# Score units of an attention kernel that end with the diagonal, and other places for its small pieces

## The chip, the cores and the metric

The kernel runs on one core of a Trainium2 chip. The metric is the device time of one execution in microseconds. Engines go by the names of the profile: PE is TensorE's matmul, PEld its weight load, DVE VectorE, ACT ScalarE, POOL GpSimd, SP SyncE.

## The reference

Input x has 2 batches of 1024 tokens with 256 channels; all is float32. An attention layer and a feed-forward layer follow each other, each added to its input and then normalised:

```python
q = (x @ Wq)  # 16 heads of 16 channels
k, v = x @ Wk, x @ Wv  # 4 heads of 16 channels, each used by 4 query heads
att = q @ k.T / 4 + slope[head // 4] * (key_pos - query_pos)
att = softmax(where(key_pos <= query_pos, att, -inf))
x = layernorm(x + (att @ v) @ Wo)
# top-1 of 8 experts (256 -> 512 -> 256, gated by silu), plus a shared expert
x = layernorm(x + shared(x) + routed(x))
```

The change concerns the attention part alone.

## The kernel before

**Tiles.** There are 2 batches of 8 query tiles (qt 0 to 7) with 128 tokens each, and key tiles of the same size. For a query tile only the keys up to its own tile count; the tile with the same number as the query tile holds the diagonal, where a part of the keys is masked.

**Two passes over the scores.** The row maximum of the softmax is taken out before the exponential, and the kernel needs it early. So it computes the scores twice.

- *S* (start_s, line 388, and end_s, line 411): queries in the partitions, keys in the free dimension, for the maximum alone. The result is reduced along the keys on VectorE into `past` (line 417). The block on the diagonal goes through the mask first: for one half of the key/value heads VectorE takes the minimum with `causal` into `diag` (line 427), for the other half ScalarE copies the block (line 435) and POOL masks it (line 438). Some slots later VectorE reduces `diag` (line 449, 128 x 1024).
- *T* (start_t, line 480, and end_t, line 494): keys in the partitions, queries in the free dimension. ScalarE evicts it with the exponential into `pT` (line 504), or, on the diagonal, copies it to `pD` (line 507), POOL masks it (line 509), and ScalarE takes the exponential later (line 521).

Between the two, join_maxima (line 456, VectorE) brings the partial maxima of a query tile together in `mneg`, and spread_maxima (line 466) turns them with four transposes (mT, line 470) and adds them to the queries on VectorE (qS, line 474).

**Units.** The S work of a query tile is cut into units (s_units, line 376): a unit is 4 key/value heads x 512 columns, that is one block of keys for all 4 query heads of a group, or two blocks for two of them, or four blocks for one. A unit with one block takes four S matmuls of 128 columns for each key/value head, one with two blocks two of 256, one with four blocks one of 512. Before the change the diagonal block is a unit by itself, and comes first.

**Steps and bursts.** The loop at line 854 goes through 72 steps, one for each pair of a query tile and a key tile. A step has two bursts: each runs two T matmuls (512 columns) and the S matmuls of two key/value heads in four row groups of the array at once, issued in turn (run, line 744). The S unit is ten steps ahead of T (LEAD): ten units run before the loop, between the projections, and the last ten steps have no S and run the pieces of the shared expert in between. Every matmul of T and S has a PSUM bank of its own from a pool of six (`ps_st`); a burst takes four.

**Slots and gaps.** After each burst stands a gap (line 795), with a running number, the slot: even slots follow the first burst of a step, odd ones the second; slots below zero are those of the lead. A gap holds, in this order: deferred work whose slot has come (after_burst), then on TensorE a product yT with the values if one is due (line 529, four matmuls, mostly in even gaps), then the transposes of maxima if the slot fits, then small pieces. The small pieces finish a query tile (finish, line 546): yq transposes the result and VectorE normalises it to y_n, ytp transposes that, o_ps multiplies it with Wo, x1tp transposes the output of the layer norm, lg makes the router's logits. They, and mT, use one bank together (`ps_m`, one buffer). Each has a cost; a gap has room 6, a product takes 4 of it, the maxima 4, and a piece its own cost and 2.

All engines but SP run in the order of the code in this part, since the schedule is manual.

Of the kernel before, what the change touches and what calls it, by code (L numbers as in the profile page):

```python
# [12 lines left out]
ALU = mybir.AluOpType  # L13
# [3 lines left out]
P = 128  # L17
N_HEAD = 16
N_KV = 4
REP = N_HEAD // N_KV  # L20
# [24 lines left out]
def attn_moe_postln_kernel(  # L45
# [15 lines left out]
    nc = tc.nc  # L61
# [9 lines left out]
    HALF = N_KV // 2  # L71
# [89 lines left out]
    causal = acon.tile([P, P], F32, tag="causal", name="causal")  # L161
# [101 lines left out]
    with (  # L263
# [111 lines left out]

        def s_units(b, qt):

            units = [(0, REP, qt, 1)]
            done = 0
            while done < qt:  # L380
                n = 4 if qt - done >= 4 else 2 if qt - done >= 2 else 1
                units += [(r, 4 // n, done, n) for r in range(0, REP, 4 // n)]
                done += n
            return [(b, qt, *u) for u in units]

        rowmax, parts = {}, {}

        def start_s(unit, h, j):
            b, qt, r0, nr, key, n = unit
            if (b, qt) not in rowmax:  # L390
                rowmax[b, qt] = (
                    mp.tile([P, N_KV, REP, P], F32, tag="diag", name="diag"),
                    mp.tile([P, N_KV, REP, 4], F32, tag="past", name="past", bufs=6),
                )
                parts[b, qt] = {qt: 0}
            parts[b, qt].setdefault(key, len(parts[b, qt]))
            g = h * HALF + j
            rows = slice(g * PAD, (g + 1) * PAD)
            sp = bank("s_ps")
            return sp, [  # L400
                lambda r=r: nc.tensor.matmul(  # L401
                    sp[:, r * n * P : (r + 1) * n * P],
                    lhsT=qT[b][rows, r0 + r, ts(qt, P)],
                    rhs=kT[b][rows, key * P : (key + n) * P],
                    start=True,
                    stop=True,
                )
                for r in range(nr)
            ]

        def end_s(unit, h, sp, last):
            b, qt, r0, nr, key, n = unit
            diag, past = rowmax[b, qt]
            gs = slice(h * HALF, (h + 1) * HALF)
            if key != qt:
                for j in range(HALF):
                    nc.vector.tensor_reduce(  # L417
                        past[:, h * HALF + j, r0 : r0 + nr, parts[b, qt][key]],
                        sp[j].rearrange("p (r k) -> p r k", r=nr),
                        AX.X,  # L420
                        ALU.max,
                        negate=True,
                    )
                return
            if not last:
                for j in range(HALF):
                    nc.vector.tensor_tensor(  # L427
                        diag[:, h * HALF + j],
                        sp[j].rearrange("p (r k) -> p r k", r=REP),
                        causal.unsqueeze(1).broadcast_to([P, REP, P]),  # L430
                        ALU.min,
                    )
            else:
                for j in range(HALF):
                    nc.scalar.copy(  # L435
                        diag[:, h * HALF + j].rearrange("p r k -> p (r k)"), sp[j]
                    )
                nc.gpsimd.affine_select(  # L438
                    out=diag[:, gs],
                    in_=diag[:, gs],  # L440
                    pattern=[[0, REP * HALF], [-1, P]],
                    compare_op=ALU.is_ge,
                    fill=MASKED,
                    base=0,
                    channel_multiplier=1,
                )
            at(
                slot + (1 + last if slot < 0 else 2 + 2 * last),
                lambda: nc.vector.tensor_reduce(  # L449
                    past[:, gs, :, 0], diag[:, gs], AX.X, ALU.max, negate=True  # L450
                ),
            )
# [3 lines left out]
        def join_maxima(b, qt):  # L456

            past = rowmax.pop((b, qt))[1]
            nc.vector.tensor_reduce(
                mnegs[qt % 2][:, :, :, ROW_MAX].rearrange("p r g -> p g r"),  # L460
                past[:, :, :, : len(parts[b, qt])],
                AX.X,
                ALU.min,
            )
# [264 lines left out]
        steps, first = [], {}  # L729
# [4 lines left out]
        slot = 0  # L734
        deferred, posts, products = [], [], []
# [4 lines left out]
        def at(when, what):  # L740

            deferred.append((when, what))
# [10 lines left out]
        def after_burst():  # L753
            for d in [d for d in deferred if d[0] <= slot]:
                deferred.remove(d)
                d[1]()
# [8 lines left out]
        def pieces(room, gap_cost=2):  # L765

            while room > 0:
                for p in posts:
                    if p[0] <= slot and p[2][0] <= room:
                        room -= p[2][0] + gap_cost if p[2][0] else 0  # L770
                        advance(p)
                        break
                else:
                    return

        def maxima():
            n = 0
            for k in order:
                if slot == 2 * first[k] - 3:
                    join_maxima(*k)  # L780
                if slot == 2 * first[k] - 2:
                    spread_maxima(*k)
                    n += 1
            return n
# [10 lines left out]
        def gap(room):  # L795
            nonlocal slot
            after_burst()
            start_route(True)
            if products and products[0][0] <= slot:
                product(*products.pop(0)[1])  # L800
                room -= 4
            room -= 4 * maxima()
            pieces(room)
            slot += 1

        def wide_gap():

            nonlocal slot
            after_burst()
            start_route(False)  # L810
            if products and products[0][0] <= slot + 1:
                product(*products.pop(0)[1])
            if not maxima():
                pieces(4, 4)
            slot += 1
            if tail:
                tail.pop(0)()
            after_burst()
            if not maxima():
                pieces(4, 4)  # L820
            slot += 1
# [21 lines left out]
        slot = -LEAD  # L843
# [10 lines left out]
        for n, (b, qt, kt) in enumerate(steps):  # L854
            last = n + 1 == len(steps) or steps[n + 1][:2] != (b, qt)
# [6 lines left out]
            if s_queue:  # L862
                unit = s_queue.pop(0)
                for h in range(2):

                    t, s = [], []
# [9 lines left out]
            else:  # L876

                t = [[start_t(b, qt, kt, h, j) for j in range(HALF)] for h in range(2)]
# [18 lines left out]
    with (  # L897
# [291 lines left out]
        h = shared(2)  # L1189
# [6 lines left out]
        for e in range(E):  # L1196
# [3 lines left out]
            else:  # L1200
                j = e + 2 - E
                rows[E + j] = fetch(E * OWN + j, 1)
            n = OWN if e + 1 < E else 1
# [8 lines left out]
            k = 4 if e == 0 else 3 if e < 3 else 2  # L1212
# [33 lines left out]
        with tc.If(n > SOON):  # L1246
            for j in range(SOON, NO):
# [3 lines left out]
                k = E + j  # L1251
# [45 lines left out]
```

## Time and profile before

| | |
|---|---|
| median of 3 runs | 600.9 us (600.33 to 602.37) |
| the profiled execution | 602.41 us, span 600.7 us |
| PE busy | 572.7 us, 95% of the span, 3708 instructions |
| DVE busy | 344.4 us, 57%, 734 instructions |
| ACT busy | 267.0 us, 44%, 484 instructions |
| POOL busy | 155.4 us, 26%, 189 instructions |
| mean granted clock of TensorE | 0.988 |
| lead (S and projections) | up to about 65 us |
| steps with S and T | about 65 to 348 us |
| steps with T alone, shared expert, router | about 348 to 450 us |
| experts | from about 450 us |

A float32 matmul appears as two instructions, one for each pass. In the chain and the timeline a line gives the start and the length in us, the engine, the tile that is written and the line of the kernel; a window's line gives its bounds, its length, then the busy time of PE, PEld, DVE, ACT and POOL with the number of instructions, TensorE's clock, the DMA share and GB/s. A group's line gives the busy time and the mean of one in ns, then the idle time before it with what ended that.

### The profile page before, as it was taken

What the parts mean: (1) busy time and instruction counts of PE and PEld (TensorE: products, weight loads), DVE (VectorE), ACT (ScalarE), POOL (GpSimd) and SP (SyncE); (2) the same over time, 40 slices, a digit from 0 to 9 for tenths busy, and PEclk for the clock granted to TensorE, in tenths of its full rate; (3) what the DMA queues carried; (4) which work ended last, traced back from release to release, by engine and by line L of the source; (5) the groups of instructions that cost most, each with busy time, mean ns of one, the idle gap of its engine ahead of it and who ended that gap; (6) DMA issues with size and microseconds to landing.
All of it is one profiled execution on the core that took longest, in us unless ns stands there. A gap on an engine that the chain in (4) does not pass through costs nothing.

```text
span 600.7 us, 9431 instructions
## 1 busy us (share of the span) xinstructions
PE 572.7 (95%) x3708; PEld 327.8 (55%) x3708; DVE 344.4 (57%) x734; ACT 267.0 (44%) x484; POOL 155.4 (26%) x189
## 2 busy tenths in 40 slices
PE   7999999999999999999999999999999999999990
PEld 4555534444445353435356644645664788888650
DVE  3186767867776767777766845342541264444541
ACT  1433476676665656655575754554112111111120
POOL 4010222111111102013321120232111237766541
PEclk9999989999999999999999999999999999999996
DMA  9700000000000000000100000100163545752100
GB/s 311 245 1 2 2 0 2 1 1 1 2 2 1 1 1 0 3 0 28 45 1 1 3 0 1 39 33 1 35 215 98 181 160 187 242 180 79 48 19 4
DMA packets 23104, 32.66 MB, mean 54 GB/s; under 512 B 3294, under 2 KB 18948, under 8 KB 23056
## 3 DMA queue, kind: packets, MB, share of 16 engines
q1 hardware_dynamic: 18784, 25.28, 12.7%
q0 software_dynamic: 3456, 6.34, 3.0%
q8 instruction: 31, 0.51, 0.4%
q10 hardware_dynamic: 816, 0.39, 0.2%
q14 instruction: 17, 0.14, 0.1%
HBM read 22.20 MB, written 12.97 MB: 59 GB/s over the span
## 4 chain that ended last, share of the span: by engine, by line
PE 87%; DVE 7%; ACT 1%; DMA 1%; issue 1%; POOL 0%; POOLq 0%; ACTq 0%
PE t_ps L485 18%; PE yT L529 11%; PE s_ps L401 11%; PE gu_sh L688 6%; PE qpj L294 5%; PE gp L1108 5%; PE dp L1124 5%; PE up L1108 5%; PE dp_sh L708 4%; DVE past L417 3%; PE o_ps L574 2%; PE mT L470 2%; DVE past L449 1%; PE lg L599 1%; PE dp L1166 1%; PE gp L1016 1%
## 5 line engine op out<-in xcount | busy, mean ns | idle before, releaser
L401 PE MATMUL s_ps<-kT,qT 32*128 32x128 f32 (+2 forms) x1280 | 184.0, 378 | 1.2 <-DVE past L417 0.7
L417 DVE TENSOR_REDUCE past<-s_ps 128x1 f32<-128x512 f32 (+2 forms) x224 | 144.6, 686 | 61.6 <-PE s_ps L401 44.9
L485 PE MATMUL t_ps<-qS,kT 32*128 32x512 f32 x576 | 173.7, 637 | 0.6 <-ACT pD L507 0.6
L504 ACT ACTIVATE pT<-t_ps 128x512 f32<-128x512 f32 x224 | 121.6, 600 | 93.2 <-PE s_ps L401 65.0
L401 PEld LDWEIGHTS s_ps<-kT,qT 32*128 32x128 f32 x1280 | 96.2, 185 | 14.4 <-ACT pT L504 4.5
L485 PEld LDWEIGHTS t_ps<-qS,kT 32*128 32x128 f32 x576 | 53.4, 183 | 63.5 <-issue 23.7
L509 POOL TENSOR_SCALAR_AFFINE_SELECT pD<-pD 128x1024 f32<-128x1024 f32 x32 | 34.8, 1093 | 101.8 <-ACT pD L507 101.6
L529 PE MATMUL yT<-pT,v 128*32 128x512 f32 x448 | 59.7, 605 | 0.0
L438 POOL TENSOR_SCALAR_AFFINE_SELECT diag<-diag 128x1024 f32<-128x1024 f32 x16 | 17.5, 1094 | 134.8 <-ACT diag L435 114.1
L233 POOL TENSOR_TENSOR rstd<-rstd,neg_half 128x1 f32<-128x1 f32 x36 | 20.6, 571 | 115.1 <-DVE rstd L232 113.3
L507 ACT COPY pD<-t_ps 128x512 f32<-128x512 f32 x64 | 34.7, 600 | 24.5 <-PE s_ps L401 13.9
L688 PE MATMUL gu_sh<-x1T,sh_gu 128*128 128x512 f32 x96 | 43.5, 596 | 0.0
L239 POOL DMA_INDIRECT slot_x<-xs,slots x32 | 32.1, 1004 | 42.0 <-DVE slots L669 24.3
L449 DVE TENSOR_REDUCE past<-diag 128x8 f32<-128x1024 f32 x32 | 38.6, 1211 | 0.0
L521 ACT ACTIVATE pD<-pD 128x1024 f32<-128x1024 f32 x32 | 33.9, 1067 | 0.2 <-POOL pD L509 0.2
L1116 ACT ACTIVATE sg<-gp 128x512 f32<-128x512 f32 x16 | 9.6, 597 | 54.6 <-PE gp L1108 54.6
L1108 PE MATMUL gp<-slot_xT,wgu 128*128 128x256 f32 x128 | 30.4, 381 | 1.2 <-ACT slot_xT L1077 1.2
L1108 PE MATMUL up<-slot_xT,wgu 128*128 128x256 f32 x128 | 30.2, 379 | 0.0
L294 PE MATMUL qpj<-xT,wq_pad 128*128 128x512 f32 x64 | 29.1, 601 | 0.1
L1124 PE MATMUL dp<-wd,slot_h 128*128 128x256 f32 x128 | 29.0, 379 | 0.0
L427 DVE TENSOR_TENSOR diag<-s_ps,causal 128x512 f32<-128x512 f32 x32 | 20.6, 685 | 13.9 <-PE s_ps L401 13.9
L1053 POOL DMA_INDIRECT zt<-z_dram,row x20 | 20.8, 1041 | 27.8 <-issue 27.8
(170 smaller groups left out, 665.7 us busy)
## 6 DMA issues: line engine op xcount, KB each, us to landing
wgu<-_L_ffn_gate_up_proj_dram SPq DMA_DIRECT2D x8, 1024.0 KB, 9.8
wd<-in_L_ffn_down_proj_dram SPq DMA_DIRECT2D x8, 512.0 KB, 5.8
slot_x<-empty SPq DMA_DIRECT2D x1, 3900.0 KB
row<-slot_x SPq DMA_DIRECT2D x8, 260.0 KB, 2.9
xs<-in_L_attn_x_dram SPq DMA_DIRECT2D x4, 512.0 KB, 7.8
z_dram<-z_sh SPq DMA_DIRECT2D x12, 128.0 KB, 1.8
row<-slot_x SPq DMA_DIRECT2D x4, 130.0 KB, 2.0
sh_gu<-L_ffn_shared_gate_w_dram SPq DMA_DIRECT2D x1, 512.0 KB
```

The costliest lines, as they stand in the source:

```text
L294: nc.tensor.matmul(dst, lhsT=w(c), rhs=xT[b][:, c, cols], start=(c == 0), stop=(c == KC - 1))
L401: lambda r=r: nc.tensor.matmul(sp[:, r * n * P : (r + 1) * n * P], lhsT=qT[b][rows, r0 + r, ts(qt, P)], rhs=kT[b][rows, key * P : (key + n ...
L417: nc.vector.tensor_reduce(past[:, h * HALF + j, r0 : r0 + nr, parts[b, qt][key]], sp[j].rearrange("p (r k) -> p r k", r=nr), AX.X, ALU.max ...
L449: lambda: nc.vector.tensor_reduce(past[:, gs, :, 0], diag[:, gs], AX.X, ALU.max, negate=True),
L485: lambda: nc.tensor.matmul(tp, lhsT=kT[b][rows, ts(kt, P)], rhs=qS[b, qt][rows].rearrange("p r q -> p (r q)"), start=True, stop=True,)
L504: nc.scalar.activation(p[:, j], tp[j], AF.Exp)
L507: nc.scalar.copy(p[:, j], tp[j])
L509: nc.gpsimd.affine_select(out=p, in_=p, pattern=[[0, HALF * REP], [1, P]], compare_op=ALU.is_ge, fill=MASKED, base=0, channel_multiplier=-1,)
L529: nc.tensor.matmul(yTs[b, qt][g * PAD : (g + 1) * PAD], lhsT=vs[b][:, kt, g, :], rhs=p[:, g, :], start=start, stop=stop,)
L688: nc.tensor.matmul(gu[k], lhsT=sh_gu[:, c, col : col + P], rhs=x1T[:, c, ts(tb, TB)], start=(c == 0), stop=(c == KC - 1),)
L1108: nc.tensor.matmul(dst[:, j], lhsT=wgu[:, e, c, col : col + P], rhs=xT[:, c, :], start=(c == 0), stop=(c == KC - 1),)
L1124: nc.tensor.matmul(dp, lhsT=h[:, f, ts(i, P)], rhs=wd[:, e, f, :], start=(f == 0), stop=(f == FC - 1),)
```

## The change

s_units no longer gives the diagonal a unit by itself: a query tile's key blocks, the diagonal's included, are cut into fours, then twos, then ones from the first key on, and the units are run in the reverse order, so that those that end with the diagonal come first. end_s reduces the blocks before the diagonal (VectorE, on 128, 256 or 384 columns for each query head) and treats the last block of such a unit as it did the diagonal before, with smaller instructions; POOL's mask and the reduction of `diag` follow once the last query heads are through.

In the gaps, joins and spreads of the maxima come one slot earlier, which puts the spreads in odd gaps. A gap with the transposes of maxima, or with a product while fewer than two query tiles are being finished, has room for a piece of cost 1 only; elsewhere a piece takes its cost and 4 of the room. In the gaps without S, deferred work comes ahead of the shared expert's piece.

```diff
         def s_units(b, qt):
-            units = [(0, REP, qt, 1)]
-            done = 0
-            while done < qt:
-                n = 4 if qt - done >= 4 else 2 if qt - done >= 2 else 1
-                units += [(r, 4 // n, done, n) for r in range(0, REP, 4 // n)]
+            units, done = [], 0
+            while done <= qt:
+                n = 4 if qt + 1 - done >= 4 else 2 if qt + 1 - done >= 2 else 1
+                units = [(r, 4 // n, done, n) for r in range(0, REP, 4 // n)] + units
                 done += n
...
-            parts[b, qt].setdefault(key, len(parts[b, qt]))
+            if key != qt:
+                parts[b, qt].setdefault(key, len(parts[b, qt]))
...
-            if key != qt:
+            has_diag = key + n == qt + 1
+            past_n = n - has_diag
+            heads = slice(r0, r0 + nr)
+            sp = [t.rearrange("p (r k) -> p r k", r=nr) for t in sp]
+            if past_n:
                 for j in range(HALF):
                     nc.vector.tensor_reduce(
-                        past[:, h * HALF + j, r0 : r0 + nr, parts[b, qt][key]],
-                        sp[j].rearrange("p (r k) -> p r k", r=nr),
+                        past[:, h * HALF + j, heads, parts[b, qt][key]],
+                        sp[j][:, :, : past_n * P],
...
+            if not has_diag:
                 return
-            if not last:
-                for j in range(HALF):
-                    nc.vector.tensor_tensor(
-                        diag[:, h * HALF + j],
-                        sp[j].rearrange("p (r k) -> p r k", r=REP),
-                        causal.unsqueeze(1).broadcast_to([P, REP, P]),
-                        ALU.min,
-                    )
-            else:
-                for j in range(HALF):
-                    nc.scalar.copy(
-                        diag[:, h * HALF + j].rearrange("p r k -> p (r k)"), sp[j]
-                    )
+            for j in range(HALF):
+                to, block = diag[:, h * HALF + j, heads], sp[j][:, :, past_n * P :]
+                if last:
+                    nc.scalar.copy(to, block)
+                else:
+                    bound = causal.unsqueeze(1).broadcast_to([P, nr, P])
+                    nc.vector.tensor_tensor(to, block, bound, ALU.min)
+            if r0 + nr < REP:
+                return
+            if last:
                 nc.gpsimd.affine_select(
...
         def maxima():
...
+                if slot == 2 * first[k] - 4:
+                    join_maxima(*k)
                 if slot == 2 * first[k] - 3:
-                    join_maxima(*k)
-                if slot == 2 * first[k] - 2:
                     spread_maxima(*k)
...
         def gap(room):
...
-            if products and products[0][0] <= slot:
+            full = bool(products) and products[0][0] <= slot
+            if full:
                 product(*products.pop(0)[1])
-                room -= 4
-            room -= 4 * maxima()
-            pieces(room)
+            if maxima() or (full and len(posts) < 2):
+                room = 1
+            pieces(room, 4)
             slot += 1
...
         def wide_gap():
...
             slot += 1
+            after_burst()
             if tail:
                 tail.pop(0)()
-            after_burst()
```

## The prediction

> **What bounds the kernel now.** I read the engine totals first, then the busy time of the stretch from 81 to 348 us (bursts with both S and T), then the chain that ended last, then the timeline around single gaps.
>
> ```profile
> PE 572.7 (95%) x3708; PEld 327.8 (55%) x3708; DVE 344.4 (57%) x734; ACT 267.0 (44%) x484; POOL 155.4 (26%) x189
> ...
> PE 87%; DVE 7%; ACT 1%; DMA 1%; issue 1%; POOL 0%; POOLq 0%; ACTq 0%
> ```
>
> ```profile
> 81.00:348.00 267.00, 263.00 (x2144) 128.17 (x2140) 196.88 (x368) 166.90 (x309) 46.91 (x49) 1.00 0.02 5
> ```
>
> TensorE seems full: 263.00 busy of 267, at a clock of 1.00. It is not. A burst of four matmuls in four row groups takes 1.07 us when nothing holds it (two passes of 0.53), a product 1.00, and the small pieces mT 0.59, yq 0.58, ytp 0.36, o_ps 1.06, x1tp 0.37, lg 0.54. The chain shows what is added:
>
> ```profile
> 206.38 1.00 PE yT L529 x8
> ...
> 208.44 1.06 PE o_ps L574 x4
> ...
> 210.58 1.00 PE yT L529 x8
> ...
> 214.93 1.00 PE yT L529 x8
> ...
> 217.00 0.37 PE x1tp L594 x2
> ...
> 219.30 1.00 PE yT L529 x8
> ```
>
> From product to product, two bursts with o_ps between take 4.20, which is their own work (2 x 1.07 + 1.00 + 1.06). With nothing between they take 4.35, a stall of 1.21; with x1tp 4.37, a stall of 0.86. So an empty gap is not faster than one with 1 us of work in it. The reason is the banks: of the four that a burst needs two are free, and its second pair waits until banks of the burst just before have been read. The program's waits are of two kinds. After a burst with narrow S matmuls the pair waits for both T banks on ScalarE, and the stall is about 1.21 minus the gap's length. After wide bursts (512 columns) it waits for one T bank and one S bank, and the stall is about 0.93 minus the gap (seven empty gaps: 0.85 to 1.13).
>
> I split slots 5 to 122 into 59 pairs (burst, odd gap, burst, even gap) and took the own durations off. 43.0 us of stall remain: empty odd gaps 11 x 1.21 and 7 x 0.93 = 19.8; ytp 9 = 8.2 (it also waits for y_n); x1tp 4 x 0.87 and 4 x 0.49 = 5.4; o_ps 2.7; a second product 2.5; yq 2.1; lg 0.31 + 0.67 = 1.0; one gap with two small pieces 1.2.
>
> That last one matters. The small pieces share one bank (the tag m):
>
> ```profile
> 122.20 0.61 PE L599 MATMUL lg<-rwT,x1T 128*128 128x8 f32 x4
> 122.26 1.08 ACT L504 ACTIVATE pT<-t_ps 128x512 f32<-128x512 f32 x2 [0.53 <-PE s_ps L401]
> 122.47 1.29 DVE L427 TENSOR_TENSOR diag<-s_ps,causal 128x512 f32<-128x512 f32 x2 [1.18 <-PE s_ps L401]
> 123.68 0.16 DVE L606 COPY logits<-lg 128x8 f32<-128x8 f32 x1
> 123.89 0.66 PE L556 MATMUL yq<-ident,y_raw 128*128 128x128 f32 x4 [1.07 <-DVE logits L606]
> ```
>
> lg's result is read only after VectorE has done the burst's two S banks, so yq behind it starts 1.7 us later and TensorE loses 1.1.
>
> **Part 1: gaps.** The order of the built programs shows what stands in each gap. The number of bursts, products and small pieces is the same, and so is SP's order of transfers; POOL's list has the same instructions, the selects on diag some places later. Only places change. After the change:
> - Empty odd gaps fall from 18 to 10: 4 of the T-bank kind, 6 of the other: 4 x 1.21 + 6 x 0.93 = 10.4. Saved 9.4.
> - x1tp alone: 2 x 0.87 + 3 x 0.49 = 3.2. Saved 2.2.
> - lg alone in seven gaps, 4 x 0.67 + 3 x 0.31 = 3.6, and in an eighth, behind a gap with x1tp only, 0.8. Added 3.4.
> - mT alone in seven odd gaps. The trace has mT only behind a product. By its 0.59, with lg's 0.54 as nearest row: 5 x 0.62 + 2 x 0.34 = 3.8; if qS (0.69 on VectorE, now behind the burst's own reductions) holds up the next S bank, up to 0.3 more each; if mT costs no more than o_ps does, 1.4 in all. I take 3.8.
> - mT and then a small piece in one gap, at slots 9, 39 and 111. The piece waits for qS on the shared bank: VectorE begins 0.27 after mT, does 1.29 (1.04 for the new units), then 0.69: 2.2 or 1.9, less mT's 0.59, gives 1.6 + 1.35 + 1.35 = 4.3, and 0.3 for slot 9's burst. Bounds: 3 x 1.1 (the lg row) to 3 x 1.9.
> - ytp alone eight times instead of nine, 7.3; o_ps 0.5; second products 2.8; yq 1.4; the gap with lg and yq gone.
>
> Sum after: 10.4 + 3.2 + 3.6 + 0.8 + 3.8 + 4.6 + 7.3 + 0.5 + 2.8 + 1.4 = 38.4. Against 43.0: **-4.6 us**.
>
> **Part 2: units.** S matmuls fall from 640 to 448 for the same columns (128 wide: 384 to 128; 512 wide: 128 to 192). A burst with 128-wide S takes 1.10 instead of 1.07, and there are 42 such before and 14 after: 28 x 0.03 = **-0.8**. Further, the fewer narrow units are why more gaps have the cheaper kind of wait; that is in part 1.
>
> VectorE gets 64 more instructions for the same columns (reductions of S 224 to 256, minima 32 to 64). The fixed part follows from these rows:
>
> ```profile
> L417 DVE TENSOR_REDUCE past<-s_ps 128x1 f32<-128x512 f32 x128 | 83.2, 685 | 35.1 <-PE s_ps L401 25.8 <-PE t_ps L485 8.8
> L449 DVE TENSOR_REDUCE past<-diag 128x8 f32<-128x1024 f32 x32 | 38.6, 1211 | 0.0
> L435 ACT COPY diag<-s_ps 128x512 f32<-128x512 f32 x32 | 17.3, 600 | 2.0 <-PE s_ps L401 2.0
> L595 ACT COPY x1T<-x1tp 128x256 f32<-128x256 f32 x16 | 6.1, 378 | 13.0 <-PE x1tp L594 13.0
> ```
>
> In a row, 512 columns take 1.285 / 2 = 0.643 and 1024 take 1.13, so 0.95 ns a column and 0.156 us fixed: 64 x 0.156 = 10.0 us. How much ends on the path? A new unit of four keys costs VectorE 1.60 in its even burst (two reductions of 384 columns, two minima of 128) and 1.04 in its odd one, 2.64 a step, where a unit without a diagonal costs 4 x 0.643 = 2.57. A step lasts about 4.3 and VectorE is busy 74% of the stretch, so most of it falls into idle time. VectorE holds 7% of the chain, 42 of its 344 us, or 12%: 10.0 x 0.12 = **+1.2**; bounds 0 and 10. Queued behind it are y_n (ytp waits for it) and qS; late next is ytp. ScalarE copies 64 small blocks instead of 32 large: by 600 ns for 512 and 378 for 256 columns, about 250 for 128, so 32 x 0.25 + 16 x 0.38 + 16 x 0.60 = 23.7 against 19.2, +4.5. They stand behind the exponentials that free the T banks; ScalarE is idle 37% of the stretch and holds 1% of the chain: **+0.1**, bounds 0 and 4.5.
>
> [...]
>
> **Part 3: the ends.** In the lead the diagonal of query tile 3 is complete three units later, so its two reductions of diag (2 x 1.13) move into slots 0 and 1, where VectorE was busy for 10.57 of the 16 us from 65 to 81 and ScalarE had hardly a pause from 72 to 80. Taken **+0.7**, a third of the 2.26, bounds -1 (mT now fills slot -1) and +2.3. In the slots without S (348 to 412 us) every block already takes its own time; some pieces change places and deferred work stands ahead of the shared expert's piece on ScalarE and VectorE, under 3.4 us of matmuls: 0, at most 0.8 (two mT behind a copy of 0.38). The joins stand one slot earlier, and no mT then waits for one: the last unit of a tile ends five slots before, and VectorE has a burst and a product (2.07) for at most 1.6 + 0.2. If a reduction of diag (1.13) stood in the same gap, mT would be 0.9 late; by the order it never does. The experts' part follows unchanged, shifted.
>
> **Sum.** -4.6 - 0.8 + 1.2 + 0.1 + 0.7 = -3.4 us. The profiled execution took 602.41 (span 600.7), 1.5 above the median of 600.9; 602.41 becomes 599.0, and the median 597.5. No change can be told within 0.3%, 1.8 us.
>
> **Rivals.**
> - *Forecast:* the stalls shrink by more than the small instructions cost: 597.5, from 594 to 599.1. Chance 0.47.
> - *More is gained:* VectorE's extra work stays hidden, mT costs its lower bound (1.4 instead of 3.8) and the three shared-bank waits 3.3 instead of 4.6: -4.6 - 2.4 - 1.3 - 0.8 + 0.7 = -8.4, 592.5. For it speaks that o_ps, a longer piece, costs at most 0.32 in seven of nine pairs. Chance 0.13.
> - *No change:* the T banks, which the change does not free any sooner, set the pace, so a piece moved into an empty gap saves nothing there and its own time alone is moved: 599.1 to 602.7. Against it: a gap with lg costs 0.31 or 0.67, an empty one 0.93 or 1.21, with own work counted apart. Chance 0.20.
> - *Slower, VectorE becomes the bound:* early query tiles (slots 0 to 30, around 81 to 155 us) and slots 104 to 121 carry many small VectorE steps (y_n, qS, layer norm) in few steps; there the extra instructions delay S reductions, and S banks hold the bursts. All 10.0 on the path gives -4.6 - 0.8 + 10.0 + 0.8 = +5.4, 606. It decides once 4.6 of the 10.0 land outside idle time (no gain left); from 6.4 the loss can be told. Against it: 70 us of idle VectorE in the stretch. Chance 0.20.
> - That the change does not do what it says is excluded by the programs' order.
>
> **Numbers.** Range: -10 (the second rival with the lead at its lower bound) to +2 leaves out most of the last rival and little else: 591 to 603. Faster 0.60, same 0.20, slower 0.20.
>
> **What would show it.** Right: S matmuls of 512 columns are the commonest, the stall sum of slots 5 to 122 is near 38, pairs with lg or mT alone in the odd gap take 3.95 to 4.4 us, and x1tp behind mT starts about 1.9 us after it. Wrong: pairs with lg that take 4.7 or more (no gain), VectorE over 15% of the chain with reductions that free S banks late (slower), or a start of the product stretch later than 79 us.

## The result and the profile after

The changed kernel took 601.64 us in the median of 12 runs (599.61 to 603.43), the kernel before 600.96 us in the runs beside it (599.92 to 603.85). The ratio is 1.0009, with a 95% interval of 0.9994 to 1.0024: no difference, where 3.4 us less had been forecast. The profiled execution took 601.33 us (span 599.6), 1.1 us less than that of before.

The page of the changed kernel, its engine totals, the chain by engine, and the groups of VectorE's reduction and of the S matmuls:

```profile
PE 566.3 (94%) x3324; PEld 309.0 (52%) x3324; DVE 347.1 (58%) x798; ACT 269.3 (45%) x516; POOL 155.2 (26%) x189
...
PE 85%; DVE 9%; ACT 1%; DMA 1%; issue 1%; POOL 0%; POOLq 0%; ACTq 0%
...
L422 DVE TENSOR_REDUCE past<-s_ps 128x1 f32<-128x512 f32 (+3 forms) x256 | 147.9, 618 | 69.7 <-PE s_ps L402 53.8
L402 PE MATMUL s_ps<-kT,qT 32*128 32x512 f32 (+2 forms) x896 | 183.8, 474 | 1.4 <-DVE diag L437 0.8
```

The program did what it was meant to do: S matmuls of 512 columns are the commonest (S has 896 instructions, two for each of 448 matmuls), VectorE has 64 more instructions for 2.7 us more of work. VectorE's share of the chain grew from 7% to 9%, far from the 15% that I had named as the sign of VectorE as the bound.

Next the busy times in windows of the changed kernel, the whole stretch first and then three pieces of 3.41 us in it:

```profile
81.00:348.00 267.00, 259.06 (x1864) 112.31 (x1862) 200.10 (x416) 171.29 (x338) 46.86 (x49) 0.99 0.02 5
264.24:267.65 3.41, 2.94 (x13) 0.74 (x12) 3.27 (x9) 1.88 (x4) 1.09 (x1) 1.00 0.00 0
267.65:271.06 3.41, 3.41 (x20) 0.72 (x16) 2.01 (x8) 0.14 (x1) 0.00 (x0) 0.50 0.00 0
271.06:274.47 3.41, 3.40 (x28) 1.52 (x23) 3.38 (x7) 2.33 (x5) 1.09 (x1) 1.00 0.00 0
```

In the middle one TensorE's clock is 0.50, and VectorE is busy for 2.01 us instead of 3.27. The stretch of before had none (clock 1.00). I call this a half-clock window. They stand at different places in the profiles (at 77, 92, 267 and 321 us, for example), and the mean clock shows that their number differs from run to run of one kernel, so a median cannot be understood without them: over the 14 profiles of this study a mean clock of .990 to .992 went with none (outside the last 15 us, where each profile has a longer one: a clock of 0.50 from 588.50 us on in the changed kernel's), .987 to .989 with one, .984 to .986 with two or one of double length. Over all runs of all kernels, each compared with its own kernel's mean, .001 of mean clock is worth 0.45 us. One window lowers the mean by 3.41 x 0.5 / 600 = .0028, so it costs about **1.3 us**. Of the changed kernel's 12 runs two lay at .988 (599.6 and 600.2 us), seven at .985 (601.2 to 602.2), three at .982 or .983 (603.3 to 603.4). Of the 23 runs of the kernel before in the next comparison ten lay at .990 to .992 (600.2 to 601.2), three at .988 (601.8 to 602.1), ten lower (602.9 to 604.1). Set against these, the changed kernel has about one window more. For the 12 runs of the kernel before beside the changed one the clock is not known; seven of them took at most 601.2 us, as the runs without a window did.

### The profile page after: what moved, and what is told of

Same layout as the page of the kernel before. It is cut to its first block, busy times and chain, and to the rows that moved or that the text cites. A ratio compares the mean times of both kernels' runs of the same rounds, so it can differ in the third digit from the quotient of the medians.

```text
span 599.6 us, 8779 instructions
## 1 busy us (share of the span) xinstructions
PE 566.3 (94%) x3324; PEld 309.0 (52%) x3324; DVE 347.1 (58%) x798; ACT 269.3 (45%) x516; POOL 155.2 (26%) x189
## 4 chain that ended last, share of the span: by engine, by line
PE 85%; DVE 9%; ACT 1%; DMA 1%; issue 1%; POOL 0%; POOLq 0%; ACTq 0%
PE t_ps L488 18%; PE yT L532 11%; PE s_ps L402 9%; PE gu_sh L691 6%; PE qpj L294 5%; PE gp L1112 5%; PE dp L1128 5%; PE up L1112 5%; PE dp_sh L711 4%; DVE past L422 4%; PE o_ps L577 2%; DVE past L452 2%; PE lg L602 1%; PE dp L1170 1%; PE gp L1020 1%; PE vpj L327 1%
## 5 line engine op out<-in xcount | busy, mean ns | idle before, releaser
L422 DVE TENSOR_REDUCE past<-s_ps 128x1 f32<-128x512 f32 (+3 forms) x256 | 147.9, 618 | 69.7 <-PE s_ps L402 53.8
L402 PE MATMUL s_ps<-kT,qT 32*128 32x512 f32 (+2 forms) x896 | 183.8, 474 | 1.4 <-DVE diag L437 0.8
L488 PE MATMUL t_ps<-qS,kT 32*128 32x512 f32 x576 | 167.9, 644 | 0.3 <-ACT pD L510 0.3
L402 PEld LDWEIGHTS s_ps<-kT,qT 32*128 32x128 f32 x896 | 79.9, 185 | 16.4 <-DVE past L422 4.7
L488 PEld LDWEIGHTS t_ps<-qS,kT 32*128 32x128 f32 x576 | 50.1, 184 | 62.6 <-issue 31.6
L434 ACT COPY diag<-s_ps 128x128 f32<-128x128 f32 (+2 forms) x64 | 21.7, 385 | 16.4 <-DVE past L422 15.1
L437 DVE TENSOR_TENSOR diag<-s_ps,causal 128x128 f32<-128x128 f32 (+2 forms) x64 | 23.9, 414 | 7.0 <-PE s_ps L402 7.0
```

Source lines behind the costliest of these rows:

```text
L402: lambda r=r: nc.tensor.matmul(sp[:, r * n * P : (r + 1) * n * P], lhsT=qT[b][rows, r0 + r, ts(qt, P)], rhs=kT[b][rows, key * P : (key + n ...
L422: nc.vector.tensor_reduce(past[:, h * HALF + j, heads, parts[b, qt][key]], sp[j][:, :, : past_n * P], AX.X, ALU.max, negate=True,)
L488: lambda: nc.tensor.matmul(tp, lhsT=kT[b][rows, ts(kt, P)], rhs=qS[b, qt][rows].rearrange("p r q -> p (r q)"), start=True, stop=True,)
```

## What the changed kernel's trace says, stage by stage

| | before, us | after, us | forecast of the difference |
|---|---|---|---|
| start of slot 5 | 80.76 (one window before it) | 80.81 (one) | +0.7 |
| slots 5 to 122 | 265.87 (none) | 264.24 (one) | -4.6 - 0.8 + 1.2 + 0.1 = -4.1 |
| from there to the start of the last dp_sh (the shared expert's last piece) | 99.99 | 100.51 | 0 |
| the rest | 154.08 | 154.05 | 0 |
| sum | 600.70 | 599.61 (-1.1) | -3.4 |

The stall sum fell from 43.0 to 41.4 us. The chain of the changed kernel shows a gap with mT alone (first column the start):

```profile
110.14 1.00 PE yT L532 x8
...
112.20 0.59 PE mT L473 x4
112.79 0.62 PE t_ps L488
...
114.13 0.99 PE yT L532 x8
```

3.99 us from product to product, no more than an empty gap takes, and mT takes the 0.59 that was read from before. The seven such pairs have 3.6 us of stall (3.8 forecast), the seven with lg 3.6 and the eighth 1.0 (3.6 and 0.8), x1tp 3.2 (3.2), the three with a piece behind mT 4.6 (4.6). The timeline of slot 39 shows that last kind:

```profile
161.46 0.66 PE L473 MATMUL mT<-ident,mneg 128*128 128x128 f32 x4
...
161.59 1.02 DVE L422 TENSOR_REDUCE past<-s_ps 128x1 f32<-128x384 f32 x2 [1.02 <-PE s_ps L402]
...
162.53 0.68 DVE L477 TENSOR_TENSOR qS<-qT,mT 128x512 f32<-128x512 f32 x1
...
163.26 0.44 PE L597 MATMUL x1tp<-ident,xs 128*128 128x128 f32 x2 [1.14 <-DVE qS L477]
```

x1tp starts 1.80 us after mT. What is not as forecast is one pair of the empty gaps, slots 87 and 88. Ten empty gaps cost 12.7 instead of 10.4, and 2.86 of it is this one. VectorE's timeline there:

```profile
261.55 1.01 DVE L634 TENSOR_TENSOR hot<-hot,first_e 128x64 f32<-128x64 f32 x1
262.48 1.27 DVE L422 TENSOR_REDUCE past<-s_ps 128x1 f32<-128x512 f32 x2
263.68 1.21 DVE L452 TENSOR_REDUCE past<-diag 128x8 f32<-128x1024 f32 x1
264.81 0.76 DVE L640 TENSOR_TENSOR cum<-cum,hot 128x8 f32<-128x8 f32 x4
265.48 1.28 DVE L422 TENSOR_REDUCE past<-s_ps 128x1 f32<-128x512 f32 x2
```

and TensorE's:

```profile
266.22 1.12 PE L402 MATMUL s_ps<-kT,qT 32*128 32x512 f32 x2 [0.47 <-DVE past L422]
```

The steps of the first routing group (route, L632 to L644 here), a reduction of diag and the reductions of S stand in one row, and the last of them frees the bank that TensorE waits for. Behind this wait begins the half-clock window of 267.65. In the kernel before the routing's long steps met the reduction of diag in slot 89, and the stall was there (1.78 us, without a window behind it). VectorE's and TensorE's lines of before:

```profile
267.28 1.21 DVE L449 TENSOR_REDUCE past<-diag 128x8 f32<-128x1024 f32 x1
268.40 1.59 DVE L637 TENSOR_TENSOR cum<-cum,hot 128x8 f32<-128x8 f32 x4
269.92 1.28 DVE L417 TENSOR_REDUCE past<-s_ps 128x1 f32<-128x512 f32 x2
```

```profile
270.65 1.12 PE L401 MATMUL s_ps<-kT,qT 32*128 32x512 f32 x2 [0.66 <-DVE past L417]
```

In the changed kernel slot 89 still has 1.09, under the half clock; lead_old (below), which has the same order from slot 5 on and no window there, has 2.31 at slot 87 and 0.52 at slot 89. Slots 87 to 90 together have 2.63 us of stall in the kernel before and 2.83 in lead_old. So this stall was not made, it was moved by two slots and gathered in one place.

## The experiments

**Theory.** The change does save stalls (up to 2 us of the median at the same clock). Its waits that remain are few and long (behind mT on the shared bank, at the routing, at the end of the lead), and a long wait is paid a second time, as a half-clock window. **Rivals:** one half of the change is a loss of its own (VectorE's small instructions take back what the gaps give); the place of the routing is to blame, in any kernel; the windows have nothing to do with the waits.

Each kernel below was timed in five rounds beside the kernel before on the same chip; ratios are to those runs (medians 602.02, 602.05 and 602.21 us in the three comparisons). The changed kernel itself was not timed again in these comparisons, so where a run is set against its 601.6 us, that run's ratio set against 1.0009 is the safer measure.

### The two halves apart

units_only has the new units and the old places of maxima and small pieces; gaps_only the reverse:

```diff
 units_only against the changed kernel
...
-                if slot == 2 * first[k] - 4:
-                    join_maxima(*k)
                 if slot == 2 * first[k] - 3:
+                    join_maxima(*k)
+                if slot == 2 * first[k] - 2:
                     spread_maxima(*k)
...
-            full = bool(products) and products[0][0] <= slot
-            if full:
+            if products and products[0][0] <= slot:
                 product(*products.pop(0)[1])
-            if maxima() or (full and len(posts) < 2):
-                room = 1
-            pieces(room, 4)
+                room -= 4
+            room -= 4 * maxima()
+            pieces(room)
 gaps_only against the changed kernel
-            units, done = [], 0
-            while done <= qt:
-                n = 4 if qt + 1 - done >= 4 else 2 if qt + 1 - done >= 2 else 1
-                units = [(r, 4 // n, done, n) for r in range(0, REP, 4 // n)] + units
+            units = [(0, REP, qt, 1)]
+            done = 0
+            while done < qt:
+                n = 4 if qt - done >= 4 else 2 if qt - done >= 2 else 1
+                units += [(r, 4 // n, done, n) for r in range(0, REP, 4 // n)]
... (start_s and end_s are those of before as well)
```

> The new units, with the old places of the small pieces and of the maxima's transposes (the deferred work of the last gaps stays ahead of the shared expert's piece). Theory A (the new gaps bring some 3 us, the new units cost about as much: VectorE's 64 more instructions, a lead that is 1.2 longer at slots -9 and -8, y_n late at slot 45): 602 to 603.5 against 601 before. Theory B (both parts are worth little alone, and what is seen after the change is an extra 3.4 us window at half clock, 1.7 us each, that depends on where VectorE holds TensorE up): within 0.6 of before in runs with as many half-clock windows, with the mean clock telling the groups apart by 1.7 us.

Measured: 600.91 us, ratio 0.999 [0.9974, 1.0006]; mean clock .990.

> The old units, with the new places of the pieces and maxima. Theory A: 597 to 598.5, the predicted gain without the cost of the units. Theory B: stall sum of slots 5 to 122 near 40.5, so about 2.5 us less, plus 1 from the transposes that fill slot -1, if no half-clock window is added; 599 to 601 if one is.

Measured: 600.32 us, ratio 0.9949 [0.9928, 0.997]; mean clock .987. Its four runs without a window took 596.7 to 597.5 us, against 600.2 to 601.2 of the kernel before: 3.4 us less at the same clock, but eight of twelve runs had windows. Two are in its profile; the lines before them are the 3.41 us ahead of each:

```profile
88.45:91.86 3.41, 1.72 (x16) 0.67 (x10) 2.90 (x8) 1.67 (x3) 0.00 (x0) 1.00 0.03 5
91.86:95.28 3.42, 3.42 (x29) 1.95 (x28) 1.16 (x2) 1.46 (x3) 0.00 (x0) 0.50 0.00 0
317.14:320.55 3.41, 1.86 (x28) 1.38 (x24) 1.88 (x3) 1.46 (x3) 0.00 (x0) 1.00 0.02 5
320.55:323.97 3.42, 3.42 (x28) 1.53 (x26) 1.29 (x2) 1.08 (x2) 0.00 (x0) 0.50 0.00 0
```

Those are slots 9 and 111, two of the three places where a piece stands behind mT, and TensorE is busy only half of the 3.41 us. Theory A had 597 to 598.5 for gaps_only and 602 to 603.5 for units_only, both missed by the medians. The gain lies in the gaps; the new units alone bring nothing that the median shows.

### The two long waits taken out of the changed kernel

route_later begins the first routing group six slots later, away from the crowded place; its matmuls rank go from gap 89 to the empty gap 95. mt_alone leaves the gap of mT to mT alone:

```diff
 route_later
-                    posts.append([slot + 1, route(routed, spread)])
+                    posts.append([slot + (7 if spread else 1), route(routed, spread)])
 mt_alone
-            if maxima() or (full and len(posts) < 2):
+            if maxima():
+                room = 0.5
+            elif full and len(posts) < 2:
                 room = 1
```

> The changed kernel with the router's VectorE steps of the first group begun six slots later (slot 91 instead of 85), away from POOL's selects at slots 85 to 89. In the changed kernel's profile this stretch (262.8 to 274.2 us) has a stall of 2.86 in one pair and a window at half clock. Theory B: that stall falls to about 0.9 to 1.2 and the half-clock window goes in nearly all runs: 1.5 to 3 us less than the changed kernel, 598.5 to 600. Theory A: the changed kernel's time, 601 to 602.

Measured: 597.24 us, ratio 0.9911 [0.9888, 0.9934]; the stall sum is 39.0 us, slots 87 and 88 have 0.85 of it instead of 2.86, and the two behind it none instead of 1.09. The forecast that the half-clock window would go in nearly all runs was wrong: four of six runs still have one by their clock, and the profile shows where, at 93.3 us behind slot 9, whose pair has 3.80 us of stall with it.

> The changed kernel with no small piece behind the transposes of maxima in a gap, so that nothing waits for qS on the shared bank at slots 9, 39 and 111. If those waits cost what the three pairs show (2.17, 1.21 and 1.24 of stall), they fall to about 0.3, 0.6 and 0.6 and the piece stands in the next gap: 2 to 2.5 us less than the changed kernel, 599 to 600. Rival (the wait only takes the place of stalls behind it): within 0.6 of the changed kernel.

Measured: 598.66 us, ratio 0.9939 [0.9919, 0.996]; stall sum 40.1. At slots 9, 39 and 111 the stall is 0.70, 0.61 and 0.64 us instead of 2.17, 1.21 and 1.24, about as expected; a window at 266.1 us, behind slot 87, is still in its profile.

Each of the two edits turns the changed kernel into one that is faster than before (by 0.9% and 0.6%). Are they one cause or two, and does the place of the routing matter by itself? Four more kernels, made of the same edits:

> The changed kernel with the routing six slots later and with no small piece behind mT in the same gap (the two edits that each gave a gain on their own: 597.2 and 598.7 where the changed kernel had about 601.6). If they save different things (the wait at the routing; three waits on the shared bank), the gains add: 594 to 595.5, 1.0 to 1.2% under the kernel before. If both only happen to avoid the same half-clock window, no more than the better one: 596.5 to 597.5.

Measured: 596.15 us, ratio 0.9891 [0.9864, 0.9919]; stall sum 35.8. Less than the sum of the two by the medians: half of its runs still have a window, in its profile at 76.9 us in the lead. The three runs without one took 594.1, 594.2 and 595.8 us, about what two separate savings would give.

> The kernel before, with only the first routing group's steps begun six slots later (its matmuls rank go from gap 89 to gap 94, both behind a product). Theory A (the changed kernel alone suffers from the place of the routing, because its extra VectorE instructions and POOL's selects fall together there): nothing to gain here, within 0.3% of the kernel before, 600 to 602. Rival B (the place of the routing is bad in any version, and has nothing to do with the change): 0.5 to 0.9% faster, 596 to 598.5.

Measured: 601.52 us, ratio 0.9983 [0.9966, 1.0]. Between the two theories: its stall at slot 89 is gone, and with one window in the run it takes 600.9 us (six runs) where the kernel before takes 602.4 (five runs), 1.5 less; but more of its runs had windows (mean clock .9867 against .9886).

> The new units in the old gaps, with the routing six slots later. Theory A: VectorE's 64 additional instructions cost time only where the routing stands among them, so the new units are freed of it: 0.3 to 0.7% under the new units alone, 597 to 599. Rival B: as much as in the kernel before with the same move. Rival C (the new units cost as much as they save wherever they stand, by VectorE's instructions all along the stretch): within 0.2% of the new units alone, 600 to 602.

Measured: 600.95 us, ratio 0.9984 [0.9969, 1.0], as units_only. There the routing had cost next to nothing (0.14 us of stall at slot 89), so nothing was to be had. Rival C's number came out; its reason is not shown by this run.

> The old units in the new gaps, with the routing six slots later (rank goes from gap 89 to the empty odd gap 95, as in the changed kernel with that move). Theory A: no extra VectorE work is there, so moving the routing saves only the stall of one empty gap (0.3 to 0.6 us): 599.5 to 600.5, 0.5 to 0.6% under the kernel before. Rival B: 0.4 to 0.9% under the gaps alone, 595 to 598. If the new units are worth something once the routing is away, this kernel is slower than the changed one with the same move (597.2).

Measured: 596.66 us, ratio 0.9906 [0.9877, 0.9934]. Theory A was wrong here: VectorE has no additional instruction in this kernel, and moving the routing still gives 3.7 us by the medians of gaps_only and of this kernel, and about 2.3 in their runs without a window (594.6 and 595.2 us against 596.7 to 597.5). The time from the start of slot 87 to that of slot 93 in the eight profiles (rank's 0.59 goes elsewhere with the move; the new gaps have o_ps's 1.06 among these slots):

| | routing as it was, us | routing later, us |
|---|---|---|
| old units, old gaps | 15.01 | 12.81 |
| new units, old gaps | 13.25 | 12.78 |
| old units, new gaps | 16.27 | 13.22 |
| both (one window in the first) | 17.31 | 13.19 |

So the routing collides with the reduction of diag in the kernel before, too, in slot 89, and in gaps_only there as well (1.66 us of stall). Only new units in old gaps happen to avoid it, and only both parts together put it into slot 87 as one long wait. Without the window both parts together take 16.25 us here (lead_old), as the old units in the new gaps do. Rival B is right that the place is bad in itself; of Theory A it remains that in the profiles a window follows the long wait in two kernels with both parts (the changed one and mt_alone) and in none of the others. The kernel is also as fast as the changed one with the same move (597.24): the new units are worth nothing here either, taken over the whole kernel.

### The windows themselves, and the lead

filler leaves every wait where it is and only gives TensorE something to do in three of them: matmuls by a block of zeros, added into yT, which is open there.

```diff
+        def idle_fill(n):
+            for _ in range(n):
+                (y,) = yTs.values()
+                nc.tensor.matmul(
+                    y[:PAD, :C], lhsT=zero[:, :PAD], rhs=wo_sb[:, 0, :], start=False, stop=False
+                )
...
+            idle_fill(3 if slot in (39, 111) else 4 if slot == 87 else 0)
             pieces(room, 4)
```

> The changed kernel with ten more matmuls by a block of zeros added into the open accumulator yT (three after mT in slots 39 and 111, four in slot 87), where TensorE otherwise waits 1.2 to 2.9 us. They change no value and nobody waits for them but TensorE's own order. Theory A (a long wait of TensorE is paid twice, the second time as a half-clock window of 3.41 us that costs 1.7, and the changed kernel has about one such window more per run than the kernel before, 2.1 against 1.2 by the mean clocks): the stalls stay as they are, no half-clock window begins after slots 39, 87 or 111, and the median falls to 599.8 to 600.8 in spite of more work. Rival B (the half-clock windows have nothing to do with these waits): clock as in the changed kernel (.985), time the same or up to 2 us more, 601.5 to 603.5.

Measured: 599.16 us, ratio 0.9959 [0.994, 0.9978]; mean clock .9901, where the changed kernel had .9849; seven of eleven runs have no window (598.6 to 599.2 us), three have one, one has two. TensorE's timeline and the busy times of two windows in that kernel:

```profile
263.20 1.91 PE L803 MATMUL yT<-wo_sb,zero 128*32 128x256 f32 x8
265.04 0.69 PE L490 MATMUL t_ps<-qS,kT 32*128 32x512 f32 x1
```

```profile
264.24:267.65 3.41, 3.41 (x25) 1.09 (x26) 3.27 (x11) 1.07 (x2) 0.31 (x1) 1.00 0.00 0
267.65:271.06 3.41, 3.34 (x28) 0.99 (x20) 3.38 (x6) 1.68 (x4) 1.88 (x2) 1.00 0.00 0
```

TensorE has 1.9 us of useless work at slot 87 and no half clock behind it. Slots 87 to 90 take 10.07 us instead of 11.40, so the window had cost 1.3 there; slots 39 and 111 each take 0.2 more. 2.5 us off the median (0.5% by the two ratios, 3 us) by adding work and shortening no wait: this run tells the waits from the windows, and the windows behind these waits are worth that much. Which of the three waits had most of it is not shown, since all three were filled at once.

lead_old has the old units for the four query tiles that are scored before slot 0:

```diff
             units, done = [], 0
+            if b == 0 and qt < 4:
+                units = [(0, REP, qt, 1)]
+                while done < qt:
+                    n = 2 if qt - done >= 2 else 1
+                    units += [(r, 4 // n, done, n) for r in range(0, REP, 4 // n)]
+                    done += n
+                return [(b, qt, *u) for u in units]
             while done <= qt:
```

> The changed kernel with the old units for the four query tiles that are scored in the lead, before slot 0; the order on TensorE is the same elsewhere. Theory A (the new units cost about 1.5 us in the lead: kernels with them started slot 5 at 79.1 to 80.6 once half-clock windows are taken off, those without at 77.5 to 79.0): slot 5 starts 1.0 to 2.0 earlier, median 599.6 to 600.6. Rival B (the difference in the lead is only where a half-clock window fell): start of slot 5 by the same correction unchanged, median within 0.1% of the changed kernel's.

Measured: 597.6 us, ratio 0.9933 [0.9908, 0.9957]. Slot 5 starts at 77.53 us, without a window. The five kernels with old units in the lead and the new gaps start it at 77.3 to 78.0, the three with new units that had no window there either at 79.4 to 79.6. The start of the lead shifts by up to 1.2 us between profiles; counted from the first S matmul, the five need 57.7 us to slot 5 and the three 59.7: the new units cost **1.9 us** in the lead. In the changed kernel VectorE and TensorE stand like this there (two views):

```profile
71.91 2.33 DVE L452 TENSOR_REDUCE past<-diag 128x8 f32<-128x1024 f32 x2
74.16 1.27 DVE L422 TENSOR_REDUCE past<-s_ps 128x1 f32<-128x512 f32 x2
75.35 1.21 DVE L452 TENSOR_REDUCE past<-diag 128x8 f32<-128x1024 f32 x1
76.48 0.17 DVE L462 TENSOR_REDUCE mneg<-past 128x16 f32<-128x32 f32 x1
```

```profile
76.71 1.11 PE L473 MATMUL mT<-ident,mneg 128*128 128x128 f32 x4 [0.35 <-DVE mneg L462]
```

and with the old units in the lead, VectorE's:

```profile
72.30 1.29 DVE L429 TENSOR_REDUCE past<-s_ps 128x1 f32<-128x512 f32 x2 [1.21 <-PE s_ps L409]
73.50 1.21 DVE L459 TENSOR_REDUCE past<-diag 128x8 f32<-128x1024 f32 x1
74.63 0.18 DVE L469 TENSOR_REDUCE mneg<-past 128x16 f32<-128x32 f32 x1
```

The two late reductions of tile 3's diag stand ahead of the reductions that free S banks and of the join that mT waits for; with the old units VectorE has 1.21 us of idle time there. The median is 4.0 us under that of the changed kernel and 2 us below the forecast. Of the 2.1 us besides the lead, 1.5 go with the clock (.9883 against .9849, at 0.45 us for .001); 0.6 are not accounted for.

The last two take everything together, with the new units from query tile 4 on, and with the old units everywhere:

> All three mended at once: old units in the lead, routing six slots later, nothing behind mT in its gap; new units from query tile 4 on. Theory A: 1.0 to 2.0 below the version with the last two (596.15), 594.1 to 595.2, the fastest of all. Rival B: 596.2, as without the old units in the lead.

Measured: 591.44 us (591.24 to 591.93), ratio 0.9826 [0.9803, 0.985].

> As the one before, but with the old units everywhere (the gaps' part of the change, routing later, nothing behind mT). It tells what the new units give from slot 0 on. Theory A (fewer waits with wide S matmuls, about 1.0 us in the stretch of slots 5 to 122, as 261.2 against 260.2 us in the two kernels with the routing later): 595.0 to 596.2, about 1 us above the version with old units in the lead only. Rival B (the new units give nothing anywhere): equal to it within 0.1%.

Measured: 591.28 us (591.21 to 591.47), ratio 0.9824 [0.9801, 0.9847]. The two are equal, so from slot 0 on the new units give nothing, and Rival B holds. In the other pairs of kernels with old and new units slots 5 to 122 differ in both directions: 264.96 us with new units against 265.87 in the old gaps (the routing's slots 87 to 92 alone give 1.76 of it), 265.12 against 264.58 there with the routing later, 261.87 against 262.93 in the new gaps with the routing later (one window in each of these two), 258.60 against 258.13 in these last two kernels. By the clock (.990 to .992) no run of either of the last two has a half-clock window outside the end, with all three long waits gone. Both are faster than expected, by 2.7 and 3.7 us at least, and the missing windows are a part of that: between the profiles of route_mt and lead_old_route_mt (594.8 and 590.2 us of span) 3.6 us lie ahead of slot 5, the lead's 1.9 and the window, and nothing in slots 5 to 122 (258.62 and 258.60); 1.0 lies behind, and its cause stays open. The totals of the second one:

```profile
PE 563.2 (96%) x3708; PEld 325.4 (55%) x3708; DVE 340.7 (58%) x734; ACT 266.7 (45%) x484; POOL 154.8 (26%) x189
```

and its window from slot 5 to slot 123:

```profile
77.30:335.43 258.13, 255.60 (x2127) 125.31 (x2123) 193.06 (x367) 168.19 (x311) 46.77 (x49) 1.00 0.02 5
```

258.13 us for what took 265.87 before. This is a version that beats both kernels: the gaps' part of the change with the routing later and mT alone, 1.76% under the kernel before.

## Why the prediction was wrong

- **Stalls, -4.6, with VectorE's +1.2 and ScalarE's +0.1: right in the sum.** The stall sum was to become 38.4 + 1.3 = 39.7; measured 41.4 with a half-clock window in it that costs 1.3, so 40.1 without (lead_old, with the same order there and no window: 40.4). The classes mT, lg, x1tp and the three shared-bank waits came within 0.2 us each. The routing's wait, 1.78 at slot 89 before and left there in my sum, went to slot 87: 2.86 there and 1.09 at 89, with the window (2.31 and 0.52 without one). ytp alone had 7.9 instead of 7.3. I had not asked what VectorE does in the slots into which its steps move, and so did not see one wait of over 2 us come up. The +1.2 was a share of 10.0 us of additional VectorE work (0.156 for each of 64 instructions); VectorE's busy time grew by 2.7 us only, 0.04 each, so that amount was too large.
- **Narrow bursts, -0.8: wrong, counted twice.** I had taken 1.07 off every burst, narrow ones too, so their 1.10 already stood in the stalls. The count was off, too: slots 0 to 123 have 36 bursts with 128-wide S before and 12 after, not 42 and 14. Old and new units are equal from slot 0 on (591.28 and 591.44).
- **Lead, +0.7: near (+0.05 in the profiles, one window in each), by two errors of opposite sign.** The new units cost 1.9 us there, near the 2.26 of the two reductions of which I took a third; and the new places of mT, the first of them in the empty slot -1, give about 1.1 (from the first S matmul to slot 5 both kernels with new units in the old gaps need 60.7 us, those in the new gaps 59.7). The start of slot 5 after 79 us, which I had named as a sign of being wrong, came (80.81), but the kernel before starts there as well (80.76).
- **The slots without S, 0, at most 0.8:** 0.5 measured.
- **The missing term: the clock.** I read the stretch's clock of 1.00 and put no price on its falling, though it can fall behind a long wait: it was 0.50 for 3.41 us behind the 2.86 us of stall at slots 87 and 88 of the changed kernel. 3.4 us forecast, 1.1 found in the profiles. The difference of 2.3 is the window (1.3), the stalls (0.4), the narrow bursts (0.8) and the slots without S (0.5), less the lead (0.65).
- **"602.41 becomes 599.0, and the median 597.5": the step that failed worst.** I carried the 1.5 us between the profiled execution and the median over as if they belonged to the profile. They were, by the times, one half-clock window, which that execution had at 77 us (clock .988) and a run at the median of 600.9 had not (later runs without a window took 600.2 to 601.2); the changed kernel's typical run has two. Of the 4.1 us between the forecast median (597.5) and the measured one (601.64), 2.3 were missing in the profile (599.0 forecast, 601.33 measured) and 1.8 in this step. At like clock the change is worth up to 2 us: with one window 599.6 to 600.2 us, against 601.8 to 602.1; with three 603.3 to 603.4, against 603.9 to 604.1. One to two windows more take all of it back.
- **The rivals.** That nothing would change came true, but not for the reason given: the T banks do not set the pace, a moved piece does save its gap. The larger gain did not come: mT and the three waits on the shared bank cost what I had taken, not their lower bounds. VectorE as the bound (all 10.0 on the path) did not come; the new units cost time for certain only in the lead. VectorE's busy time in slots 5 to 122 is 197.69 us with 48 more instructions against 195.75 before: 0.04 us for each of them, less than the 0.156 of my sum, and it does not show in the time of the kernel (591.44 and 591.28 us with new and old units from slot 0 on).

## What to carry to other kernels

When a profile shows few long waits instead of many short ones, look at the granted clock in the rows behind each of them (here 0.50 for 3.41 us, about 1.3 us a window), and compare runs by their mean clock before comparing medians; a profiled execution that lies off its median may have one half-clock window more or less (1.5 us for the kernel before, with one at 77 us). A part that moves small pieces moves everything that is queued behind them: for each step that arrives in a new slot, add up what the engine it runs on already has there. Try the parts of a change one by one: here one part is worth 0.5% alone, 1.8% with two small repairs, and the other nothing, with a loss in the lead.

## What the runs showed of the hardware

- **The clock.** Half-clock windows last 3.41 us, and they begin on a grid of that length: in the changed kernel's profile the clock falls to 0.50 at 76.50, 267.65 and 588.50 us (the last is the longer one at the end), 191.15 and 320.85 us apart, which is 56.0 and 94.0 times 3.413 us; in that of gaps_only two windows begin 228.7 us apart (67.0 times). The 3.41 us ahead of half-clock windows had TensorE busy for 1.72 and 1.86 us (gaps_only) or even 2.94 us (the changed kernel from 264.24 us). Other stretches of the same grid in the changed kernel's profile had less and were followed by full clock: 2.28 us busy from 161.83 to 165.25 us and 2.26 from 318.85 to 322.26, each with a clock of 1.00 in the 3.41 us behind it. So busy time alone does not decide; what does is not shown by these runs. That the same kernel has none to three windows (mean clocks from .993 to .983 in the runs of the kernel before) fits a grid that falls differently against the waits in each run.
- **VectorE behind POOL.** L634 on 128x64 took 1.01 us, where its neighbour L632 of the same shape took 0.21 (both are steps of the routing). POOL's timeline in the changed kernel:

```profile
261.39 1.09 POOL L441 TENSOR_SCALAR_AFFINE_SELECT diag<-diag 128x1024 f32<-128x1024 f32 x1 [15.13 <-ACT diag L434]
266.43 1.09 POOL L512 TENSOR_SCALAR_AFFINE_SELECT pD<-pD 128x1024 f32<-128x1024 f32 x1 [3.95 <-ACT pD L510]
```

  L634 ends at 262.56, when POOL's select has ended (262.48), and the four steps of cum that meet the second select (266.43 to 267.52) take 1.47 where the four ahead of them took 0.76. The kernel before has the same in its trace: the four steps at 268.40, which meet POOL's select of 268.49, take 1.59, and the four at 262.81, which meet none, 0.76. In route_later L634 takes 0.22 and each four of cum 0.76. The traces show that these long steps and the selects fall together; why is not shown.
